# Two layers of cross-attention: the first image tokens of two entries in one tile of values

## The chip, the cores and the metric

The kernel runs on one core of a Trainium2 chip. The metric is the device time of one execution in microseconds (us), the median over some runs. A run's span, as the profiler shows it, goes from the first to the last instruction; the time has a little more around it.

The engines have these names in the profile: PE is TensorE's matmul, PEld its weight load, DVE VectorE, ACT ScalarE, POOL GpSimd, and SP the queue of SyncE, which issues nearly all DMAs of this kernel.

## The reference

B = 16 entries of S = 256 positions and C = 320 channels, in 20 heads of 16, pass through two layers. Each entry has 256 context tokens of E = 512 channels. In layer 0 the first 77 are text and the other 179 image tokens:

```python
q = hidden_states @ Wq
k_text, v_text = text @ Wk, text @ Wv
text_out = softmax(q_h @ k_h.T * scale) @ v_h
ip_k, ip_v = ip @ Wk_ip, ip @ Wv_ip
scores = q_h @ ip_k_h.T * scale
text_probs = softmax(q @ k_text.T * scale)            # over all channels, one per entry
sem = (text_probs @ text) @ ip.T * scale              # shared by the 20 heads
ip_probs = softmax(scores + 0.5 * sem) * spatial_mask[:, None]
out = (text_out + ip_probs @ ip_v_h) @ Wout + bout + residual
```

Layer 1 has 252 text tokens and 4 image tokens and normalises the two sides of its semantic term. All is in fp32.

## The kernel before

Each fp32 operand is split into a high and a low float32r half, and a product is the sum of three terms (high·high, high·low, low·high). So `prod` with kt = 4 blocks of 128 context channels issues 12 matmuls (line 325). The halves are made by `halves`: ACT copies the high half (L244), another engine subtracts (L245).

Layer 0 works on pairs of entries c = (2c, 2c+1), which share one context tile for each of the four blocks: `cta`, `cta`, `ctb`, `ctb`, each 128 x 2 halves x 512 columns, entry after entry, 77 text columns first in each. `context` loads the four raw blocks, one DMA of 128x512 each, and POOL and ACT split them. For each pair the tasks are:

- `keys0` (task k0): three blocks m of keys; for m = 0, 1 a product of the text columns (two entries by 96 columns, L325) and one of the image columns (two by 180), for m = 2 one product of all 512. The keys go through `kst` to memory, `kd`, by `keys_out`.
- `queries0` (q0), to memory `qd`.
- `tokens0` (m0t): the product of an entry's 77 text tokens with its image tokens, 77 x 192; its half, M, is part of the semantic term.
- `values0_` (v0): three products per entry, 128 tokens by 320 channels: tokens 0 to 127 with the text weights (`wC`), tokens 0 to 127 with the image weights (`wD`), tokens 128 to 255 with the image weights. ACT evacuates each into `vr`, the first two with a mask on the rows (`tmask`), with a column of ones after each head's 16 (V0W = 17 columns a head).
- `semantic0` (s0): the text probabilities of an entry; its first product is queries by text keys, 128 x (2 x 96) (L792), with the keys read back from `kd` into `kb`.
- `close0` (c0): the output projection (L725).

The attention itself runs in 80 slots, five groups g of four heads for each entry. A slot's K stack `ks` has 77 rows of M (broadcast to the four heads by ACT, L846), 48 rows of keys loaded from `kd`, and two rows of indicators (-1 for text, -1 for image columns); its Q stack `qs` has the text probabilities (ACT, L843), the queries, and the negative maxima. `stacks0` fills them, LEAD = 4 slots ahead. In a slot, `score0` makes S (L874), DVE takes the maxima (L875, L876), PE transposes them (L881), `turned0` makes the transposed scores T (L896), ACT their exp P (L899), POOL the product with the semantic factor rs (L902), and `attend0` the products with the values (L934). L820 is a product of an entry's semantic task.

PE runs in program order. What comes between a slot's own steps is set by the table STEPS: for each task the times, in slots, at which its steps are issued (negative: before the entry's first slot); `fill` runs the steps that are due. In layer 0 SP's instructions, too, stand in an order set when the program is built. The start, up to the first slot, is written out by hand in `begin`.

```python
def prod(out, lhs, rhs, kt):
    terms = [(k, a, b) for k in range(kt) for a, b in ((0, 0), (0, 1), (1, 0))]
```

## Time and profile before

| what | us |
|---|---|
| median of 3 runs (lowest, highest) | 1452.26 (1450.29, 1454.2) |
| the profiled execution, its time | 1451.59 |
| the profiled execution, its span | 1449.8 |
| busy: PE | 1401.7 |
| busy: PEld | 1157.8 |
| busy: DVE | 1174.2 |
| busy: POOL | 1152.3 |
| busy: ACT | 937.6 |

A row of a timeline has the start, the time, the engine, the line of the code, the operation, the tiles (out<-in), the shapes and how many instructions were merged; in brackets the idle time ahead of it and what ended that. The ends of matmuls are modelled, so the time of a run of matmuls is taken from its start to the start of what follows. A row of a group has the count, the busy us and the mean ns of one, and the idle time ahead of them. Layer 0 ends, and layer 1 begins, between 565 and 690 us.

### The profile page before, as it was taken

How to read it: one execution, taken by the hardware profiler on the slowest of the kernel's cores; microseconds unless marked ns; L12 is line 12 of the kernel's file. 1: busy time of each engine (PE TensorE's matmuls, PEld its weight loads, DVE VectorE, ACT ScalarE, POOL GpSimd, SP SyncE). 2: the span in 40 equal slices, each digit the busy share in tenths (PEclk: the TensorE clock that was granted, in tenths of full speed). 3: DMA queues.
4: the chain of work that ended last, by engine and by line, in shares of the span. 5: the costliest groups of instructions: out<-in, count | busy, mean ns of one | idle time of the engine just before them, and what ended most of it. 6: DMA issues, size and time to landing. Idle time of an engine off the chain costs nothing.

```text
span 1449.8 us, 35042 instructions
## 1 busy us (share of the span) xinstructions
PE 1401.7 (97%) x12166; PEld 1157.8 (80%) x12166; DVE 1174.2 (81%) x2570; ACT 937.6 (65%) x2075; POOL 1152.3 (79%) x1181
## 2 busy tenths in 40 slices
PE   7899999999999999889999999999999999999998
PEld 6788888888888888577777788878878888888865
DVE  5477777777777788867888888988998889888887
ACT  5567676767676776755666666666666666566553
POOL 4269797979787878887778887788778877887785
PEclk9999999999999999999999999999999999999999
DMA  6866575665656578575544444544454445444411
GB/s 200 197 161 181 143 186 147 163 169 155 168 151 171 145 201 232 133 188 155 158 123 124 143 141 125 154 137 140 130 150 138 139 135 149 139 136 131 130 33 50
DMA packets 236284, 215.74 MB, mean 149 GB/s; under 512 B 57834, under 2 KB 222732, under 8 KB 236108
## 3 DMA queue, kind: packets, MB, share of 16 engines
q1 hardware_dynamic: 233886, 212.53, 53.4%
q8 instruction: 97, 1.59, 0.5%
q10 hardware_dynamic: 2222, 0.98, 0.3%
q14 instruction: 79, 0.65, 0.2%
HBM read 127.32 MB, written 85.16 MB: 147 GB/s over the span
## 4 chain that ended last, share of the span: by engine, by line
PE 52%; DVE 3%; POOL 1%; issue 1%; ACT 0%; DMA 0%; ACTq 0%; DVEq 0%; POOLq 0%
PE X L1075 18%; PE X L325 9%; PE X L725 6%; PE P L1088 5%; PE T L1018 4%; PE S L1023 3%; PE P L1090 2%; PE X L1209 1%; PE X L651 1%; PE P L1055 1%; DVE mn L1024 1%; PE P L934 1%; POOL P L902 0%; DVE wt L1078 0%; POOL wt L1066 0%
## 5 line engine op out<-in xcount | busy, mean ns | idle before, releaser
L902 POOL TENSOR_TENSOR P<-P,rs 128x512 f32<-128x512 f32 x320 | 412.4, 1313 | 136.1 <-ACT P L899 136.0
L1075 PE MATMUL X<-ctb,gm 128*128 128x512 f32 x1120 | 293.3, 403 | 0.7 <-DVE wt L1078 0.7
L1066 POOL TENSOR_TENSOR wt<-P,ctb 128x512 f32<-128x512 f32 x212 | 268.1, 1293 | 0.0
L899 ACT ACTIVATE P<-T 128x512 f32<-128x512 f32 x320 | 174.7, 594 | 101.8 <-PE T L896 83.7
L1024 DVE TENSOR_REDUCE mn<-S 128x4 fp32r<-128x1008 f32 x160 | 192.1, 1200 | 58.7 <-PE S L1023 56.8
L1075 PEld LDWEIGHTS X<-ctb,gm 128*128 128x128 f32 x1120 | 202.5, 190 | 38.5 <-DVE wt L1078 0.9
L1078 DVE TENSOR_TENSOR wt<-X,wt 128x512 f32<-128x512 f32 x240 | 159.7, 682 | 4.2 <-PE X L1075 3.9
L1030 ACT ACTIVATE P<-T 128x512 f32<-128x512 f32 x212 | 115.2, 598 | 58.3 <-PE T L1018 56.6
L1080 POOL TENSOR_TENSOR wt<-wt 128x512 f32<-128x512 f32 x80 | 103.5, 1294 | 60.2 <-DVE wt L1078 60.0
L876 DVE TENSOR_REDUCE mn<-S 128x4 fp32r<-128x716 f32 x160 | 142.5, 890 | 0.0
L1065 ACT ACTIVATE ctb<-P 128x512 fp32r<-128x512 f32 x212 | 122.4, 625 | 29.4 <-PE X L1075 20.6
L934 PE MATMUL P<-P,vr 128*32 128x256 f32 x1920 | 123.7, 388 | 0.0
L725 PE MATMUL X<-ho,wF 128*128 128x256 f32 x768 | 109.0, 286 | 2.2 <-DVE ho L974 1.2
L725 PEld LDWEIGHTS X<-ho,wF 128*128 128x128 f32 x768 | 100.5, 189 | 8.8 <-DVE ho L974 2.7
L725 PE MATMUL X<-hq,wE 128*128 128x256 f32 x720 | 102.7, 286 | 4.6 <-ACT hq L706 3.3
L725 PEld LDWEIGHTS X<-hq,wE 128*128 128x128 f32 x720 | 96.4, 193 | 8.3 <-ACT hq L706 3.8
L875 DVE TENSOR_REDUCE mn<-S 128x4 fp32r<-128x308 f32 x160 | 74.8, 468 | 23.2 <-PE S L874 22.9
L945 DVE STREAM_TRANSPOSE nt<-P 128x512 f32<-128x512 f32 x80 | 57.1, 714 | 39.2 <-PE P L934 38.9
L934 PEld LDWEIGHTS P<-P,vr 128*32 128x32 f32 x1920 | 56.1, 110 | 40.8 <-issue 4.9
L874 PE MATMUL S<-ks,qs 125*128 125x256 f32 x480 | 85.7, 301 | 2.2 <-DMA ks<-kd 1.7
L874 PEld LDWEIGHTS S<-ks,qs 125*128 125x128 f32 x480 | 64.4, 189 | 28.2 <-issue 24.1
L325 PE MATMUL X<-cta,wA 128*128 128x252 f32 (+3 forms) x534 | 78.8, 292 | 7.9 <-ACT wA L244 5.7
(231 smaller groups left out, 3275.3 us busy)
## 6 DMA issues: line engine op xcount, KB each, us to landing
qd<-q SPq DMA_DIRECT2D x80, 256.0 KB
qs<-qd SPq DMA_DIRECT2D x160, 112.0 KB
ks<-kd SPq DMA_DIRECT2D x160, 112.0 KB
rawc<-in_cT_dram SPq DMA_DIRECT2D x60, 256.0 KB
kd<-kst SPq DMA_DIRECT2D x50, 256.0 KB
qs<-qd SPq DMA_DIRECT2D x60, 192.0 KB
ks<-kd SPq DMA_DIRECT2D x60, 192.0 KB
qd<-q SPq DMA_DIRECT2D x64, 128.0 KB
```

What stands on the lines that cost most here:

```text
L325: last = mm(out, lhs(a, k), rhs(b, k), start=i == 0, stop=i == len(terms) - 1)
L725: mm(pp, w(s, k, slice(m * 128, (m + 1) * 128)), a[:, t], start=i == 0, stop=i == len(terms) - 1)
L874: mm(sp[:, h], Q[: XROW + T0, h, t * 128 : (t + 1) * 128], K[: XROW + T0, h], start=True, stop=True)
L876: anchor(nc.vector.tensor_reduce(mn[:, 1, :, t], sp[:, :, T0:], axis=AX.X, op=ALU.max))
L899: exp = anchor(nc.scalar.activation(pt, st[p], AF.Exp, scale=SCALE))
L902: anchor(nc.gpsimd.tensor_mul(pt, pt, rs[:, t : t + 1].to_broadcast([128, 2, S])))
L934: mm(pv[32 * s : 32 * s + 32, o : o + S], v[:, vt, h : h + 32], P[k, s // 2][:, t, s % 2], start=vt < 2, stop=vt != 1,)
L1024: anchor(nc.vector.tensor_reduce(maxes[k + 2][:, :, t], sp[:, :, :T1], axis=AX.X, op=ALU.max))
L1065: nc.scalar.activation(R[k, u][:, t], P[k, u][:, t], AF.Copy, scale=0.5)
L1066: anchor(nc.gpsimd.tensor_sub(W[k, u][:, t], P[k, u][:, t], f(R[k, u][:, t])))
L1075: mm(yp, gm[:, gb], R[k, u][:, kt], start=i == 0, stop=i == len(blocks[n]) - 1)
L1078: nc.vector.tensor_mul(product, yp, w[:, n])
```

## The change

**The layout of a pair.** The context tile of a pair is PW = 538 columns wide: the even entry's text (0 to 76), the odd entry's image tokens (77 to 255), a gap of 26, the even entry's image tokens (282 to 460), the odd entry's text (461 to 537). In this layout 128 columns from 205 hold 51 image tokens of the odd entry, the gap, and 51 of the even one. `bring` loads a raw block of a pair with three DMAs (77, 179 and 256 columns); the first pair's is loaded in one DMA and put in place by the halves.

**Values.** The tile at 205 gives the first image values of both entries with one product, which ACT evacuates twice, with a mask for each, into both entries' `vr`. So a pair has five products where it had six, starting at columns 0, 410, 77, 205 and 333. `attend0` of the even entry makes sure that this product has been issued.

**Text keys and tokens.** The text keys' product has 156 columns (was 192), the tokens' 180 (was 192), the semantic product 154 (was 192). The text keys are evacuated in two pieces, one for each entry. An odd entry now has image tokens ahead of text in its keys.

**The stacks.** The two indicator rows lie in `kd`, written there at the start by six DMAs from memory to memory; a K stack loads 50 rows instead of 48, and nothing is copied from `mt` to `ks`. M is broadcast over all 256 columns (1024 with the four heads, was 716).

**Steps.** Numbers of STEPS moved, among them those of v0, m0, w7, t1 and o1. The opening loads wki ahead of the first wq and xq ahead of wv.

```diff
+GAP = 2 * T0 - 128
+PW = 2 * S + GAP
+CT, CI = (PW - T0, 0), (T0, S + GAP)
...
-    "m0e": (-7.4,),
-    "m0o": (-4.8,),
+    "m0e": (-8.2,),
+    "m0o": (-4.6,),
     "v0e": (-7, -5.2, -4.8,),
-    "v0o": (-4, -3.8, -3.4,),
+    "v0o": (-4.6, -4.4, -3.2,),
...
-    "t1": (-3.2, -2.2, -2.2, -1.4, -0.2,),
+    "t1": (-3.2, -2, -2, -1.2, 0,),
...
-    ("m0t", 2): (1.6,),
+    ("m0t", 2): (4.4,),
...
+    def bring(raw, src):
+
+        if src.shape[-1] == 2 * S:
+            for to, at, n in (0, 0, T0), (T0, S + T0, NI), (S + GAP, T0, S):
+                dma(raw[..., to : to + n], src[..., at : at + n])
+        else:
+            dma(raw, src)
...
-    ind0 = buf("raw", [128, 512], bufs=SIZES["RAW"], name="ind0")[:2, :S]
-    dma(ind0, ind0_d)
-    ind0r = buf("mt", [8, S], FR, name="ind0r")[:2]
-    nc.scalar.copy(ind0r, ind0)
+    for r in range(2):
+        for j, pieces in ((0, ((IM[0], IM[1]), (TX[0], TX[1]))), (1, ((slice(0, S), slice(0, S)),))):
+            for to, at in pieces:
+                rows = kd[0][:, (XROW + r) * H : (XROW + r + 1) * H, j, to]
+                dma(rows, ind0_d[r : r + 1, at].unsqueeze(1).to_broadcast([B // 2, H, to.stop - to.start]))
...
-        dma(ks[i][KS0 - 2 : KS0], ind0r.unsqueeze(1).to_broadcast([2, 4, S]))
...
+    def text_keys(c, kst, w, n):
+
+        kp = bank()[:n, : 2 * T0 + 2]
+        prod(kp.rearrange("p (b t) -> p b t", b=2), w, lambda s, k: of_pair(c, k, s, CT[1], CT[0] - CT[1] - 1, T0 + 1), 4)
+        text_rows(kst, (kp[:, :T0], kp[:, T0 + 2 :]), slice(0, n))
...
     def values0_(b):
-        ct, i = ct0[b // 2], b % 2
-        V = vr[(b + 2) % 3]
-        for t, (w,), lo, sc in ((0, wv0, 0, tmask[:, 0:1]), (1, wvi0, 0, tmask[:, 1:2]), (2, wvi0, 128, 1.0)):
+        j, ring = 1 - b % 2, lambda b: vr[(b + 2) % 3]
+        V = ring(b)
+        parts = [(0, wv0, (PW - 128, 0)[j], 1), (2, wvi0, (CI[0], CI[1] + NI - 128)[j], 0)]
+        nc.vector.tensor_copy(vcols(V, V0W)[:, 0:2, :, 16], vmasks[j].unsqueeze(2).to_broadcast([128, 2, H]))
+        if b % 2:
+            parts.insert(0, (1, wvi0, S + T0 - 128, 1))
+        for t, (w,), lo, masked in parts:
             vp = bank()[:, :320]
-            prod(vp, lambda s, k: ct(s, k)[:, i, lo : lo + 128], lambda s, k: w(s, k), 4)
-            nc.scalar.activation(
-                vcols(V, V0W)[:, t, :, 0:16], vp.rearrange("p (h d) -> p h d", d=D), AF.Copy, scale=sc
-            )
+            prod(vp, lambda s, k: ct0[b // 2][k][:, s, lo : lo + 128], lambda s, k: w(s, k), 4)
+            for i in (j,) if t != 1 else (1, 0):
+                scale = vmasks[i][:, t : t + 1] if masked else 1.0
+                nc.scalar.activation(
+                    vcols(ring(b - i if t == 1 else b), V0W)[:, t, :, 0:16], vp.rearrange("p (h d) -> p h d", d=D), AF.Copy, scale=scale
+                )
+            if t == 1:
+                results["mixed", b // 2] = True
             yield
         return V
...
     def semantic0(b):
...
-        NT = 96
+        NT = T0
...
-                dma(K[T0 : T0 + XROW], stack_rows(kd[0][b // 2][:, :, b % 2])[:, hs])
+                dma(K[T0 : T0 + XROW + 2], kd[0][b // 2][:, 1 - b % 2].rearrange("(q h) t -> q h t", h=H)[:, hs])
...
-                    m = f(get("m0t", b)[:, 0:1, T0:]).to_broadcast([T0, 4, S - T0])
-                    order(nc.scalar.copy(K[:T0, :, T0:], m), *casts[-1:])
+                    m = f(get("m0t", b)[:, 0:1]).to_broadcast([T0, 4, S])
+                    order(nc.scalar.copy(K[:T0], m), *casts[-1:])
...
     def attend0(k):
         b, g = divmod(k, NG)
         v, pv = get("v0", b), bank("P")
+        while ("mixed", b // 2) not in results:
+            step(("v0", b + 1))
```

Where instructions come to stand is shown at three places. First PE, in the steady part of layer 0, where the tokens and values of an odd entry are made; each row is an instruction of one term or several, `cta` and `ctb` the blocks of the context, `wC` and `wD` the text and image weights of the values, P the product of the attention. Before:

```order
L874 MATMUL S<-ks_193,qs_189 128x256 x4
L896 MATMUL T<-qsl,ksl 128x256 x4
L325 MATMUL X<-cta_82 77x192 x3
L325 MATMUL X<-cta_83 77x192 x3
L325 MATMUL X<-ctb_84 77x192 x3
L325 MATMUL X<-ctb_85 77x192 x3
L325 MATMUL X<-wD,cta_82 128x320 x3
L325 MATMUL X<-wD,cta_83 128x320 x3
L325 MATMUL X<-wD,ctb_84 128x320 x3
L325 MATMUL X<-wD,ctb_85 128x320 x3
L934 MATMUL P<-P_95,vr 32x256 x2
```

After:

```order
L346 MATMUL X<-cta_82 77x180 x3
L346 MATMUL X<-cta_83 77x180 x3
L346 MATMUL X<-ctb_84 77x180 x3
L346 MATMUL X<-ctb_85 77x180 x3
L346 MATMUL X<-wD,cta_82 128x320 x3
L346 MATMUL X<-wD,cta_83 128x320 x3
L346 MATMUL X<-wD,ctb_84 128x320 x3
L346 MATMUL X<-wD,ctb_85 128x320 x3
L346 MATMUL X<-wC_177,cta_82 128x320 x3
L346 MATMUL X<-wC_177,cta_83 128x320 x3
L346 MATMUL X<-wC_177,ctb_84 128x320 x3
L346 MATMUL X<-wC_177,ctb_85 128x320 x3
```

The wD product that opens the odd entry's values is now the one of both entries, and the wC product follows it at once; over layer 0 the rows with wD go from 384 matmuls to 288.

Second the queue of SP in the opening, from the last weight loads to the first keys on their way to memory (`mt` held the indicator rows, `kst` keys, `q` queries). Before:

```order
L139 DMA raw<-in_wvi_dram 128x320
L139 DMA ind_196<-in_ind_dram 2x256
L139 DMA ks_192<-mt_198 2x4x256
L139 DMA ks_193<-mt_198 2x4x256
L139 DMA ks_194<-mt_198 2x4x256
L139 DMA ksl<-mt_198 2x4x256
L139 DMA kd_66<-kst_237 128x2x256
L139 DMA kd_66<-kst_237 128x256
```

After:

```order
L145 DMA kd_66<-in_ind_dram 8x20x256
L145 DMA raw<-in_wv_dram 128x320
L145 DMA kd_66<-in_ind_dram 8x20x179 x2
L145 DMA kd_66<-in_ind_dram 8x20x77
L145 DMA raw<-in_wvi_dram 128x320
L145 DMA kd_66<-in_ind_dram 8x20x77
L145 DMA rawc_92<-in_wvi_dram 128x320
L145 DMA rawc_93<-in_wvi_dram 128x320
L145 DMA raw<-in_wvi_dram 128x320
L145 DMA xq_144<-in_xT_dram 128x3x256
L145 DMA kd_66<-kst_254 128x2x256
```

The indicator rows now go to `kd` between the loads of the value weights, and nothing stands between the last of these loads and the keys but one load of x.

Third the queue of SP in a steady pair, where the context of a later pair is loaded between the loads of the stacks. Before:

```order
L139 DMA rawc_93<-in_cT_dram 128x512
L139 DMA rawc_92<-in_cT_dram 128x512
L139 DMA qd_2626<-q_299 128x2x256
L139 DMA qd_2626<-q_299 128x256
L139 DMA ks_193<-kd_66 48x4x256
L139 DMA qs_189<-qd_1997 48x1024
```

After:

```order
L145 DMA rawc_93<-in_cT_dram 128x256
L145 DMA rawc_93<-in_cT_dram 128x179
L145 DMA rawc_93<-in_cT_dram 128x77
L145 DMA rawc_92<-in_cT_dram 128x256
L145 DMA rawc_92<-in_cT_dram 128x179
L145 DMA rawc_92<-in_cT_dram 128x77
L145 DMA qd_2651<-q_322 128x2x256
L145 DMA ks_213<-kd_66 50x4x256
L145 DMA qs_209<-qd_1974 48x1024
```

Six loads stand where two stood, ahead of the loads of the next stacks.

209 lines of the change are left out of this document (123 added, 86 removed), and 26 rows, old and new, of the table STEPS.

## Prediction

> **What bounds the kernel now.** I read the head of the page first, then the table by stretches, then the waits of the middle of layer 0, and last the timeline of TensorE (PE) and of the DMA queue (SP) at the places which the change touches. The head shows PE busy for 97% of the span, in front of DVE (81%), the weight loads (PEld, 80%) and POOL (79%).
>
> ```profile
> span 1449.8 us, 35042 instructions
> PE 1401.7 (97%) x12166; PEld 1157.8 (80%) x12166; DVE 1174.2 (81%) x2570; ACT 937.6 (65%) x2075; POOL 1152.3 (79%) x1181
> ```
>
> The table by stretches (core, then busy us and instructions of PE, PEld, DVE, ACT, POOL; then granted clock, DMA share, GB/s) tells where PE is the limit and where it isn't.
>
> ```profile
> 0.00:50.00 50.00, 37.91 (x227) 35.34 (x228) 24.29 (x65) 28.13 (x63) 17.80 (x37) 0.97 0.72 202
> 50.00:100.00 50.00, 44.06 (x368) 38.18 (x367) 34.04 (x70) 29.98 (x69) 25.26 (x21) 0.97 0.71 187
> ...
> 200.00:300.00 100.00, 100.00 (x932) 86.48 (x934) 74.78 (x183) 72.08 (x162) 86.88 (x78) 1.00 0.66 176
> ...
> 500.00:600.00 100.00, 94.83 (x883) 80.30 (x884) 82.03 (x196) 72.14 (x166) 81.24 (x77) 0.98 0.75 199
> 600.00:700.00 100.00, 89.44 (x807) 71.96 (x807) 75.83 (x159) 58.17 (x126) 79.96 (x79) 0.98 0.59 158
> 700.00:800.00 100.00, 96.22 (x796) 76.36 (x795) 89.08 (x177) 64.57 (x142) 81.82 (x86) 1.00 0.49 139
> ```
>
> In the middle of layer 0 PE has no gap at a clock of 1.00, so work taken off PE there is time. The opening leaves PE idle for 18 us, the transition between the layers (500 to 800) for 19.5 us; there, work on PE is worth only what the gaps don't swallow. A chain of other engines could hide behind a full PE, so I looked at who waits for whom from 200 to 500 (us in total, times, longest).
>
> ```profile
> POOL P L902 <- ACT P L899: 44.8, 44, 2.4
> ACT P L899 <- PE T L896: 43.6, 40, 1.8
> ```
>
> POOL waits for ACT and ACT for PE: the chain of a slot has its slack behind PE, not ahead of it. PE sets the pace.
>
> **The value products.** The timeline of PE in a steady pair (start, us, engine, line, names, shapes, count) prices one product.
>
> ```profile
> 302.04 0.29 PE L820 MATMUL X<-tph,M 77*128 77x256 f32 x1
> ...
> 308.11 0.70 PE L325 MATMUL X<-cta 128*77 128x192 f32 x6
> 308.64 0.69 PE L325 MATMUL X<-ctb 128*77 128x192 f32 x6
> 309.17 1.07 PE L325 MATMUL X<-wC,cta 128*128 128x320 f32 x6
> 310.08 1.04 PE L325 MATMUL X<-wC,ctb 128*128 128x320 f32 x6
> 310.95 0.22 PE L881 MATMUL X<-ident_r,mn 128*16 128x128 f32 x1
> ...
> 315.56 1.48 PE L792 MATMUL X<-kb,q 128*128 128x192 f32 x12
> 316.88 0.22 PE L881 MATMUL X<-ident_r,mn 128*16 128x128 f32 x1
> ...
> 526.77 0.28 PE L820 MATMUL X<-tph,M 77*128 77x256 f32 x1
> ```
>
> A value product starts at 309.17 and the next instruction at 310.95: 1.78 us for 12 matmuls of 320 columns, 148 ns each. Six products a pair become five, so a pair gives back 1.78 us. The two L820 rows lie six entries (three pairs) apart, so a pair takes 224.73/3 = 74.9 us.
>
> **Tokens, text keys, semantic scores.** The token product (12 matmuls, 77 weight columns, 192 moving) takes 309.17 − 308.11 = 1.06 us; at 180 columns, in proportion, 0.07 us less, twice a pair: 0.13 us. Text keys go from 192 to 156 columns and semantic scores from 192 to 154, 24 matmuls of each a pair. The semantic product L792 takes 316.88 − 315.56 = 1.32 us for the same 192 columns which cost the token product 1.06. What differs is the weights, 128 columns against 77: at 128 weight columns a short product is paced by its load, not by the columns that stream. So I count nothing for the shorter columns there. The bounds are 0 and the token product's rate, 1.06/12/192 = 0.46 ns a column: 24 × (36 + 38) × 0.46 = 0.82 us a pair. I take 0, since L792 is the product itself and the token rows only its neighbour.
>
> Together 1.9 us a pair. Seven pairs (the second to the eighth) are computed under a full PE, or nearly so: 13.3 us. The eighth pair's products fall partly into 500 to 600, where PE idles 5.17 us, so up to 1.9 of the 13.3 is less sure. The first pair's is in the opening, below.
>
> **What is added in the steady stretch.** The groups by form (count, then busy us and mean ns) price it.
>
> ```profile
> L843 ACT CAST qs<-tph 77x1024 fp32r<-77x1024 f32 x48 | 49.8, 1039 | 0.0
> L846 ACT CAST ks<-M 77x716 fp32r<-77x716 f32 x48 | 37.7, 785 | 0.0
> ...
> L245 POOL TENSOR_TENSOR cta<-rawc,cta 128x512 fp32r<-128x512 f32 x44 | 56.1, 1294 | 0.0
> ```
>
> The copy of M into the K stack grows from 716 to 1024 columns, so to the L843 row: 8 a pair by 254 ns, 2.0 us. With three more split key evacuations ACT gets about 2.7 us a pair; it goes from 72% of 74.9 to some 78% of 73. POOL's context halves grow by 26 of 512 columns: 4 × 66 ns = 0.26 us a pair; POOL goes from 87% to about 89%. DVE's share stays below 80%. None reaches PE's share, and the cover is the 44 us that POOL and ACT wait for each other in 300 us. If the cover fails, the exps come late and PE waits for P. I allow 1 us for new stalls, 0 to 4 over the layer.
>
> SP issues three context loads for each one: 8 more a pair by about 0.45 us (0.91/2, in the rows below), 3.6 us of issue in 73. Behind them in the queue stand the K and Q loads of the stacks, each well ahead of its use, as the timeline shows:
>
> ```profile
> 308.30 0.33 SPq L139 DMA_DIRECT2D ks<-kd  x1
> ...
> 316.93 0.69 PE L874 MATMUL S<-ks,qs 125*128 125x256 f32 x4
> ```
>
> 8.6 us from issue to use. A burst of three context loads in place of one is 0.9 us more, two such bursts 1.8; that fits.
>
> **The opening.** SP issues in a row here, and PE waits twice for its loads.
>
> ```profile
> 24.51 2.29 SPq L139 DMA_DIRECT2D ks<-mt  x3
> ...
> 33.20 3.65 SPq L139 DMA_DIRECT2D kd<-ho x6
> ...
> 38.36 0.33 SPq L139 DMA_DIRECT2D ks<-kd  x1
> ...
> 40.92 0.91 SPq L139 DMA_DIRECT2D rawc<-in_cT_dram  x2
> 42.63 1.63 SPq L139 DMA_DIRECT2D raw<-in_cT_dram  x2
> 45.24 3.67 SPq L139 DMA_DIRECT2D kd<-kst  x4
> 49.01 3.74 SPq L139 DMA_DIRECT2D kd<-ho  x6
> 52.86 0.70 SPq L884 DMA_DIRECT2D qs<-mt  x1
> ...
> 44.16 0.71 PE L874 MATMUL S<-ks,qs 125*128 125x256 f32 x4 [1.67 <-DMA ks<-kd]
> ...
> 54.96 0.71 PE L896 MATMUL T<-qs,ks 127*128 127x256 f32 x4 [3.13 <-DMA qs<-mt]
> ```
>
> The indicator copies ks<-mt (2.29 us and one more) leave this place, and six DMAs from memory to memory take over earlier, between the weight loads. Each kd<-ho group has four issues for six, 1.2 us less (3.65/6 × 2). The first S follows ks<-kd and can come 1.2 us earlier, up to 3 if the removed copies also held up the queue; PE's wait there is 1.67, so no more than that is gained at once. The first T follows qs<-mt, which has stood behind the context loads and both key groups: 1.2 to 1.7 earlier by the first S, 1.2 by the shorter group, 8 × 0.35 to 0.45 = 2.8 to 3.6 later by the longer loads, of which the queue's own pauses between 41.83 and 45.24 (1.8 us free of issues) cover all or nothing. That is −1.9 to +1.2 for T. The pair's product saved, 1.78, lies ahead of this wait and counts only if T's wait vanishes. The six memory copies are the unknown: at one to two issues (0.45 to 0.9 us) behind wv or wvi they delay a value product, which has room until 44. I take −1 for the opening, nearer the early end since the pauses are there, and from −4 to +3.
>
> **Moved steps.** Numbers of STEPS move by up to 2.8 slots (m0t of entry 2) but mostly by a few tenths; a step moved under a full PE changes who is first, not the sum. In the transition and in layer 1 the products are the same ones in another order: 0, from −2 to +2. The steps of the mixed product are pulled ahead of the first value step of the even entry, so the odd entry's ring buffer is taken early; three buffers serve two entries, and the next taker comes five slots later.
>
> **The sum.** The profiled execution took 1451.59 us. −13.3 − 1 + 1 + 0 = 1438.3; the median of the three runs is 0.67 above the profiled execution, so 1439.0 us. A difference of about 0.3%, 4.4 us, is what a measurement of this kernel can tell from none: faster means under 1447.9, slower over 1456.6.
>
> **The rivals.**
>
> The first: *odd weight columns.* The mixed tile and two others begin at columns 205, 77 and 333 of a 4-byte tile, where before all began at 0 or 128. If such a load took longer, 36 matmuls a pair would pay. At twice the 110 ns (1.32/12) by which L792 is paced, a matmul would take 220 ns for 148: 36 × 72 = 2.6 us a pair against 1.9 saved. That is 7 × 0.7 = +4.9, about 1457. It cancels the gain from 53 ns a load. Against it stand the rows of the attention products, whose weights start at multiples of 17 columns in layer 0 (half of them odd) and of 22 in layer 1 (all even):
>
> ```profile
> L934 PEld LDWEIGHTS P<-P,vr 128*32 128x32 f32 x1920 | 56.1, 110 | 40.8 <-issue 4.9 <-POOL hq L707 1.0 <-POOL P L902 0.3
> ...
> L1088 PEld LDWEIGHTS P<-P,v1t 128*32 128x32 f32 x848 | 22.1, 109 | 16.5 <-issue 0.4
> ```
>
> 110 against 109 ns: odd starts cost nothing at 32 columns. Chance 0.05.
>
> The second, the one on the slower side: *the K load gets late.* It carries 50 rows where it carried 48. Its only bound in the rows is the first one, issued at 38.36 and waited for until 44.16: 5.8 us at most. The steady cushion is 8.6. So a load half as long again (8.7) just uses it up, and each further 0.2 us in some 70 slots eats the whole 13.3. At 1.6 times, 9.3 us, S is 0.7 late in each slot: 49 us on top of 1439, about 1488. For it: the DMA share is 0.66 already, and the last step of the score hangs on it. Against: 5.8 includes the wait for the writes of kd, so the load is shorter. Chance 0.06. The Trainium skill, "DMA: Bandwidth & Descriptors", section "Why a DMA increments its semaphore by 16 and not by 1", says that a transfer runs on the largest number of engines up to 16 that divides its slowest dimension: 48 rows on 16, 50 on 10, the factor 1.6 by estimate. No row of this profile shows the number of engines of one load.
>
> The third: *shorter columns pay after all.* The 0.82 us of the upper bound by 7 pairs is 5.7 us more: 1433. Against it stands the 1.32 of L792. Chance 0.09. The Trainium skill, "TensorE: Matmul & The Clock Gate", section "Back-to-back issue gap", gives N/2.4 + 2.5 ns for N columns alone, which would say 82 ns at 192, and adds that at small N it undercounts for want of the load; L792 agrees with the addition, at 110.
>
> The fourth: *the transition takes the gain back.* Layer 0 ends 13 us earlier, while the casts of layer 1's weights and contexts on ACT, POOL and DVE, which PE waits for between 500 and 800, don't come earlier: if half of the gain returns as idle time, 1446; if all, 1452. For it: 19.5 us of idle are there now. Against: no other engine is above 90% in these stretches, and the same steps are due by slot, so they move up with the layer. Chance 0.14, half of it within 0.3%.
>
> **Chances and range.** The forecast has 0.66. Faster: 0.66 + 0.09 + 0.07 = 0.82. Same: 0.07 + 0.03 of the first rival = 0.10. Slower: the rest of the first, 0.02, and the second, 0.06: 0.08. The forecast's own range is 1434 to 1446 by the opening (−4 to +3), the stalls (0 to 4) and the transition (±2). To leave out two in ten I reach to the third rival below and to the fourth above: 1430 to 1449.
>
> **What would show it.** In the profile after, the two wD groups of L325 have 144 matmuls where these have 192:
>
> ```profile
> L325 PE MATMUL X<-wD,cta 128*128 128x320 f32 x192 | 33.7, 310 | 0.0
> L325 PE MATMUL X<-wD,ctb 128*128 128x320 f32 x192 | 33.3, 309 | 0.0
> ```
>
> The pair's period falls from 74.9 to about 73.0, with PE still at 100% between 200 and 500. The 12 matmuls of a product at an odd column still take 1.78 us; 2.6 would show the first rival. Twelve semantic matmuls still take about 1.3; 1.1 would show the third. Any wait of PE for ks<-kd after 100 us would show the second. Idle time of PE from 500 to 800 well above 19.5 us would show the fourth. The first T should come at 53 to 55; a T past 58 would mean that I took the context loads too lightly. A wait of PE on P (L902) in the steady stretch would say that ACT's 2.7 us were not hidden.

## The result: slower by 1.2%

The changed kernel takes 1469.78 us (median of 4 runs, 1468.62 to 1472.09) against 1453.08 before (4 runs beside it, 1450.29 to 1454.2): a ratio of 1.0119, 95% interval 1.0100 to 1.0139. The forecast was 1439.0, from 1430 to 1449, with 0.82 on faster. The sign was wrong.

The profiled execution has a span of 1466.8 us against 1449.8. The head of its page:

```profile
span 1466.8 us, 34987 instructions
PE 1396.1 (95%) x12070; PEld 1149.3 (78%) x12070; DVE 1193.0 (81%) x2618; ACT 951.4 (65%) x2106; POOL 1152.4 (79%) x1185
```

PE has 96 matmuls fewer and 5.6 us less busy time, and yet the span is 17 us longer: PE waits more. The table by stretches, with the columns of the one before, shows where:

```profile
0.00:50.00 50.00, 32.89 (x195) 30.20 (x196) 23.60 (x77) 28.31 (x70) 17.84 (x41) 1.00 0.70 192
50.00:100.00 50.00, 41.69 (x328) 37.47 (x327) 30.33 (x62) 26.06 (x62) 17.83 (x15) 0.90 0.70 186
...
200.00:300.00 100.00, 96.78 (x921) 82.26 (x919) 76.35 (x181) 73.48 (x163) 86.28 (x77) 1.00 0.65 173
...
500.00:600.00 100.00, 95.53 (x882) 81.84 (x883) 80.19 (x189) 74.56 (x166) 81.81 (x76) 0.98 0.77 204
600.00:700.00 100.00, 88.92 (x819) 69.96 (x816) 80.08 (x171) 63.87 (x138) 85.23 (x84) 0.97 0.61 159
700.00:800.00 100.00, 94.75 (x774) 74.83 (x772) 82.94 (x161) 59.56 (x128) 77.21 (x81) 0.97 0.44 130
```

From 200 to 300 PE was full before and now idles 3.2 us. The opening idles 25.4 us (18 before), at a mean clock of 0.95 (0.97 before). From 500 to 800 it idles 20.8 (19.5 before), at a clock lower by up to 0.03.

Where the time goes is read best from the starts of the same slots, taken from the first matmul of T in each (us; 60 is the first slot of the thirteenth entry, 90 lies behind the transition):

| slot | before | after | later by | of it since the row above |
|---|---|---|---|---|
| 0 | 54.96 | 60.94 | +5.98 | +5.98 |
| 5 | 102.20 | 108.54 | +6.34 | +0.36 |
| 20 | 213.88 | 220.64 | +6.76 | +0.42 |
| 60 | 510.87 | 524.52 | +13.65 | +6.89 |
| 90 | 761.82 | 779.00 | +17.18 | +3.53 |
| 159 | 1418.61 | 1436.54 | +17.93 | +0.75 |
| end of the span | 1449.81 | 1466.84 | +17.03 | −0.90 |

So there are three losses: 6 us in the opening, 7 in four steady pairs (75.97 us for one against 74.24), 3.5 in the transition. The waits of PE from 200 to 500 (us in total, times, longest) had no row before and now have three, each once a pair:

```profile
PE X L346 <- DVE tmp L1029: 5.6, 4, 1.4
PE X L346 <- DVE ho L1050: 2.4, 4, 0.6
PE P L1012 <- POOL P L977: 2.3, 4, 0.6
```

In starts of matmuls these are gaps of 1.72, 0.87 and 0.97 us, where before no gap above 0.33 stands. Less the 0.15 to 0.3 that lies between two starts anyway, they cost 2.7 to 3.1 us a pair. The products save 1.9, and a pair is 1.7 longer, so some 0.5 to 0.9 us of the loss stand in no gap of this size.

### The copy that waits for POOL

The first of the three waits on the timelines of PE, DVE and POOL in the changed kernel:

```profile
338.09 1.06 PE L346 MATMUL X<-wD,ctb 128*128 128x320 f32 x6
340.55 1.11 PE L346 MATMUL X<-wC,cta 128*128 128x320 f32 x6 [1.40 <-DVE tmp L1029]
```

```profile
334.78 1.35 DVE L570 COPY vr<-vmask 128x40 f32<-128x40 f32 x1 [0.22 <-PE P L1012]
336.03 0.70 DVE L1023 STREAM_TRANSPOSE nt<-P 128x512 f32<-128x512 f32 x1
...
340.00 0.41 DVE L1029 TENSOR_TENSOR tmp<-nt,P 128x256 f32<-128x256 f32 x1
340.33 0.41 DVE L1050 TENSOR_TENSOR ho<-X,ho 128x256 fp32r<-128x256 f32 x1
```

```profile
334.77 5.02 POOL L977 TENSOR_TENSOR P<-P,rs 128x512 f32<-128x512 f32 x4 [0.41 <-ACT P L974]
```

PE waits at 340.55 for DVE, by its row until the operation on `tmp` is done; DVE has worked without a pause since 334.78. At the head of that chain stands a copy of 40 elements a partition, 1.35 us long. It starts with the first of POOL's four operations (334.77), and DVE's next instruction starts at 336.03, when that operation (5.02/4 = 1.26) ends. The second wait has the same form: the copy takes 1.22 from 299.62, and POOL's two operations run from 298.26 to 300.79.

```profile
299.62 1.22 DVE L570 COPY vr<-tmask 128x40 f32<-128x40 f32 x1 [0.47 <-PE P L1012]
300.75 0.22 DVE L259 TENSOR_TENSOR kst<-X,kst 128x77 fp32r<-128x77 f32 x1
```

```profile
298.26 2.53 POOL L977 TENSOR_TENSOR P<-P,rs 128x512 f32<-128x512 f32 x2 [0.63 <-ACT P L974]
```

All sixteen copies by their source line (shortest, median, longest ns, then first and last start):

```profile
L570 DVE COPY vr<-tmask x8: 194/1216/1228, 14.4 to 528.7; 128x40 f32<-128x40 f32 x8
L570 DVE COPY vr<-vmask x8: 196/1347/1351, 49.1 to 565.6; 128x40 f32<-128x40 f32 x8
```

The copy by itself takes 0.2 us: so long last the two that meet an idle POOL, at 39.98 and 49.14. Thirteen start while POOL works on a product P (L977), and every one of them ends 0.06 to 0.07 us after that operation, also the three that start late in it and last only 0.48 to 0.70 us. This is the line of the diff that fills the column of ones, `nc.vector.tensor_copy(vcols(V, V0W)[:, 0:2, :, 16], ...)`, once for each entry.

### The profile page after: what moved, and what is told of

Its sections match the earlier page's. It is cut to its first block, busy times and chain, and to the rows that moved or that the text cites. A ratio compares the mean times of both kernels' runs of the same rounds, so it can differ in the third digit from the quotient of the medians.

```text
span 1466.8 us, 34987 instructions
## 1 busy us (share of the span) xinstructions
PE 1396.1 (95%) x12070; PEld 1149.3 (78%) x12070; DVE 1193.0 (81%) x2618; ACT 951.4 (65%) x2106; POOL 1152.4 (79%) x1185
## 4 chain that ended last, share of the span: by engine, by line
PE 80%; DVE 8%; DMA 3%; POOL 3%; issue 2%; ACT 2%; SPq 1%; ACTq 0%; DVEq 0%; POOLq 0%
PE X L346 17%; PE X L1153 17%; PE X L798 11%; PE P L1012 7%; PE S L948 5%; PE P L1166 5%; PE T L1096 4%; PE T L971 4%; PE S L1101 3%; PE P L1168 2%; POOL P L977 1%; SPq L145 1%; PE X L1287 1%; DVE mn L951 1%; POOL wt L1144 1%
## 5 line engine op out<-in xcount | busy, mean ns | idle before, releaser
L977 POOL TENSOR_TENSOR P<-P,rs 128x512 f32<-128x512 f32 x320 | 410.2, 1306 | 139.9 <-ACT P L974 139.7
L1012 PE MATMUL P<-P,vr 128*32 128x256 f32 x1920 | 126.9, 386 | 5.7 <-POOL P L977 4.8
L346 PE MATMUL X<-wC,cta 128*128 128x320 f32 x480 | 81.0, 315 | 7.0 <-DVE tmp L1029 7.0
```

What stands on the lines that cost most here:

```text
L346: last = mm(out, lhs(a, k), rhs(b, k), start=i == 0, stop=i == len(terms) - 1)
L977: anchor(nc.gpsimd.tensor_mul(pt, pt, rs[:, t : t + 1].to_broadcast([128, 2, S])))
L1012: mm(pv[32 * s : 32 * s + 32, o : o + S], v[:, vt, h : h + 32], P[k, s // 2][:, t, s % 2], start=vt < 2, stop=vt != 1,)
```

## The experiments

Most of these kernels were executed once, and their times are compared with one execution of the kernel before on the same chip (1450.88 to 1452.45; for the indicator copies with the median of 16, 1452.84). How far they carry is seen from the last kernel, which was profiled twice: its slots 20 to 60 took 292.50 and 292.52, its slot 5 came at 109.43 and 107.17, its stretch from slot 60 to 90 took 255.18 and 257.53, and that from 90 to 159 657.28 and 658.81. So a steady pair is good to 0.02 us, the opening and the transition only to about 2.4, layer 1 to about 1.5.

### The copy of the ones: on ACT, and alone on DVE

```diff
-        nc.vector.tensor_copy(vcols(V, V0W)[:, 0:2, :, 16], vmasks[j]...
+        nc.scalar.copy(vcols(V, V0W)[:, 0:2, :, 16], vmasks[j]...
```

> The changed kernel with one edit: the copy that sets the column of ones in vr runs on ACT, not on DVE. Theory A: in the changed kernel this copy of 40 elements takes 1.2 to 1.35 us on DVE in the steady part of layer 0 (0.19 us in the opening), and the evacuations behind it on DVE free the banks of PSUM late; the two gaps of PE that follow it (1.72 us ahead of a wC product, 0.87 ahead of a wB product, 2.3 us a pair over their usual 0.15) go, a pair falls from 75.97 to about 73.7 us, and the run from 1470 to about 1456. Theory B (the moved steps make the evacuations late): the gaps stay, a pair stays at 76.0, 1470. A copy on ACT of 1 us or more would say that the place of the writing, not DVE, costs the time.

Measured: 1459.22, 10.6 under the changed kernel's median and 3 above what was expected. The pair goes from 75.97 to 73.94. The copies take 0.25 us, and of the three waits from 200 to 500 the two behind DVE's chain are gone:

```profile
L570 ACT COPY vr<-tmask x8: 251/254/265, 14.4 to 522.4; 128x40 f32<-128x40 f32 x8
L570 ACT COPY vr<-vmask x8: 243/257/267, 48.9 to 559.9; 128x40 f32<-128x40 f32 x8
```

```profile
PE P L1012 <- POOL P L977: 2.4, 4, 0.6
PE S L948 <- DVE mn L951: 1.8, 4, 0.5
```

The other way round, the kernel before with such a copy added for each entry:

```diff
         V = vr[(b + 2) % 3]
+        nc.vector.tensor_copy(vcols(V, V0W)[:, 0:2, :, 16], tmask[:, 0:2].unsqueeze(2).to_broadcast([128, 2, H]))
```

> The kernel before with one part of the change alone: a copy on DVE of 40 elements a partition into the columns of ones of vr, once an entry (the same values that stand there already). Theory: on DVE it takes 1.2 us and more while POOL works, and PE, which is full here, gets waits of up to 2 us a pair: a pair of 75 to 76.3 instead of 74.24, 1456 to 1465. Rival (the copy only hurts with the change's other order): the copy takes 1.2 us, but a pair stays at 74.3, 1453.

Measured: 1454.06 against 1452.45, a pair of 74.73 (+0.49): under the 75 of the theory, above the 74.3 of the rival.

```profile
L504 DVE COPY vr<-tmask x16: 196/207/1467, 15.3 to 557.4; 128x40 f32<-128x40 f32 x16
```

Here eight of the copies meet an idle POOL and take 0.2 us; five last 1.46, and these too end 0.06 us after one of POOL's operations. So the copy costs what the place of POOL's operation makes of it: 2.0 us a pair in the changed kernel, 0.5 in the one before.

### The moved steps

`STEPS` of the kernel before in the changed kernel; then the same with the ones on ACT.

> The changed kernel with the table STEPS of the kernel before, all else changed. Theory A (copy on DVE): a pair in the steady part keeps gaps of PE of some 2 us or more, near 76 us; layer 1, whose work is the same, goes back to 48.1 us an entry from 48.4 if its own numbers of STEPS made the difference: some 4 us less there, 1466. Theory B (moved steps): a pair falls to about 72.4 us (74.24 less 1.9), and the run to about 1452.

> The copy on ACT as in e1, and the table STEPS of the kernel before. If the moved steps cost something in the steady part, a pair falls below e1's 73.95, to 72.4 to 73.3, and layer 1 runs at 48.1 us an entry instead of 48.4. If they are worth something now that DVE is free of the copy, a pair is at 74 or more. In the run with before's STEPS alone a pair took 75.3 against 75.97, so I expect about 73.3 and, with an opening later by 3 us, the same time as e1: 1459.

Measured: 1472.61 and 1467.06 (1466 and 1459 were expected); pairs of 75.28 and 74.69 on average from slot 20 to 60. With the old table the steady pair is 0.7 faster beside the DVE copy and 0.75 slower without it, so the moved numbers aren't the loss. But they set what the copy costs: with the old table it is worth 0.6 us a pair (75.28 to 74.69), with the new one 2.0. Layer 1, slots 90 to 159, goes back from 657.54 to 656.68 and 656.71 (656.79 before): its 0.75 us are the moved steps. All seven executions here with the old table took 655.4 to 656.8 there, all thirteen with the new one 657.2 to 658.8.

### POOL's gap

The third wait stands behind POOL: after two halves of the context (L259) it does four products P in a row, and PE waits for the last.

```profile
358.31 2.64 POOL L259 TENSOR_TENSOR ctb<-rawc,ctb 128x538 fp32r<-128x538 f32 x2
360.92 0.45 POOL L1034 TENSOR_TENSOR hsn<-tmp 128x128 f32<-128x128 f32 x1
361.34 5.20 POOL L977 TENSOR_TENSOR P<-P,rs 128x512 f32<-128x512 f32 x4
```

Two attempts, both with the ones on ACT. One issues a step of k0 later (−12 to −11.4), the other lets DVE subtract the last of a pair's four halves:

```diff
-                halves(*ahead.pop(0), eng, wait)
+                last = eng is nc.gpsimd and i == len(parts) and parts[-1][0].shape[-1] == 2 * S
+                halves(*ahead.pop(0), nc.vector if last else eng, wait)
```

> The copy on ACT as in e1, and one number of STEPS moved: the fifth time of k0 from -12 to -11.4, so that POOL's two halves of ctb don't stand next to each other. In e1 a pair takes 73.95 us, with a gap of PE of 0.97 us ahead of a P matmul that waits for POOL, behind these two halves (2.64 us), and one of 0.82 where S waits. Theory (POOL's own order makes the rest of the loss): the 0.97 gap goes and the pair falls to about 73.2 us. Rival (POOL has simply no slack over these slots: 9.4 us of work in the slot of 9.1): the wait moves to another place and the pair stays at 73.9.

> The copy on ACT as in e1, and the low half of a pair's last context block made on DVE, not on POOL. In e1 POOL is busy for 22.6 us in three slots of 22.45 (slots 47 to 49), behind two halves in a row. Theory (POOL is the bound there): with 1.3 us less on POOL the gap of 0.97 ahead of a P matmul goes, and perhaps part of the 0.82 one: a pair of 72.8 to 73.3 instead of 73.95. Rival (the wait isn't POOL's amount of work): 73.9 or more.

The later step gave 1472.18 and pairs of 76.5, where 73.2 was hoped for: PE now waits at the text keys for that half, and DVE runs late behind it.

```profile
PE X L346 <- DVE sp L869: 4.6, 3, 1.5
PE X L956 <- DVE mn L951: 3.0, 3, 1.0
PE X L346 <- POOL ctb L259: 2.6, 4, 0.7
```

The half on DVE took the wait for POOL away; pairs of 73.13, 0.8 less than with the ones on ACT alone. One row is left from 200 to 500:

```profile
PE S L949 <- DVE mn L952: 1.8, 4, 0.5
```

Its time, 1459.16, is nonetheless that of the kernel with the ones on ACT (1459.22): the 3.2 us won from slot 20 to 60 are lost by slot 20 (+1.8) and from 60 to 90 (+1.7), both inside what two executions of one kernel differ by.

### The opening

SP in the opening of the changed kernel, from the loads of pair 1's context to the first load for T:

```profile
43.45 6.69 SPq L145 DMA_DIRECT2D rawc<-in_cT_dram  x6
50.51 3.52 SPq L145 DMA_DIRECT2D raw<-in_cT_dram  x6
54.08 1.95 SPq L145 DMA_DIRECT2D kd<-kst  x4
56.07 2.59 SPq L145 DMA_DIRECT2D kd<-ho  x4
58.76 0.77 SPq L959 DMA_DIRECT2D qs<-mt  x1
```

The twelve context loads hold SP from 43.45 to 54.03, 10.6 us, where four held it from 40.92 to 44.26. The issues themselves are not longer, 0.33 to 0.43 us each; between them SP waits for earlier DMAs to land (its waits from 43 to 59):

```profile
SPq L145 <- DMA ks<-kd: 4.3, 3, 1.8
SPq L145 <- DMA qs<-qd: 1.0, 2, 0.7
SPq L145 <- DMA xq<-in_xT_dram: 0.5, 1, 0.5
```

In both programs a DMA of SP waits on the semaphore that it is going to use, until the DMA eight places ahead of it in the queue has landed; these pauses end 0.016 us after that landing. Before, the same waits (for ks<-kd, qs<-qd and xq) came partly behind the context loads, among the key writes, so the loads cost less than it looks: from its first load of K to qs<-mt SP takes 17.24 us (41.52 to 58.76) where it took 14.50 (38.36 to 52.86), 2.7 us more. The other 3.2 us are there before that first load. The shorter key group takes 2.59 for 3.74, the 1.2 us less that were foretold; so the eight more loads cost some 3.9. PE's waits follow, 3 us later on ks<-kd and 6 on qs<-mt:

```profile
47.19 0.71 PE L948 MATMUL S<-ks,qs 125*128 125x256 f32 x4 [2.06 <-DMA ks<-kd]
...
60.94 1.19 PE L971 MATMUL T<-qs,ks 127*128 127x256 f32 x4 [6.13 <-DMA qs<-mt]
```

Two kernels put one part each into the kernel before: three DMAs for each context load, and six copies of the indicator rows (into a spare place in memory).

```diff
-                dma(raw, src)
+                if shape[-1] == 2 * S:
+                    for lo_, hi_ in ((0, T0), (T0 + S, 2 * S), (T0, T0 + S)):
+                        dma(raw[..., lo_:hi_], src[..., lo_:hi_])
+                else:
+                    dma(raw, src)
```

```diff
+    spare = dram.tile([B // 2, 2 * H, 2, S], F32, name="spare")
+    for r in range(2):
+        for j, pieces in ((0, (slice(0, S - T0), slice(S - T0, S))), (1, (slice(0, S),))):
+            for to in pieces:
+                dma(spare[:, r * H : (r + 1) * H, j, to], ind0_d[r : r + 1, to]...
```

> The kernel before with one part of the change alone: each context load of the pairs after the first is issued as three DMAs (77, 179 and 256 columns) into the same contiguous place. Theory (loads): the four loads of the opening then take 6 to 10 us of SP instead of 2.5, qs<-mt stands behind them, and the first T comes at 58 to 61 instead of 54.96; slot 5 comes 4 to 6 us late (106 to 108 instead of 102.2); in the steady part a pair stays at 74.24. 1456 or so. Rival (the opening's loss comes from the other edits there): T at 56 or earlier, slot 5 at 103, 1452.

> The kernel before with one part of the change alone: six copies of the indicator rows from memory to memory, of the change's sizes, into a spare place that nothing reads, among the value weights' loads; ks<-mt stays as it was. Theory (their 0.65 MB delay what is loaded behind them): the last load of wvi, for which ACT waits 3.06 us before (until 23.67), lands 2 to 4 us later, the first S at 46 to 48 instead of 44.16, slot 5 1 to 3 us late; 1453 to 1456. Rival (the copies are free, and the q of the changed kernel is late by ACT's order alone): first S within 1 us of 44.16, slot 5 within 1 us of 102.2.

The split loads: 1455.89, first T at 59.91 (+4.95), slot 5 +4.8, a pair 74.24, as the theory had them; from the first load of K to qs<-mt SP takes 19.46 us. SP's rows:

```profile
40.86 5.46 SPq L139 DMA_DIRECT2D rawc<-in_cT_dram  x6
47.24 4.55 SPq L139 DMA_DIRECT2D raw<-in_cT_dram  x6
```

The indicator copies: 1459.8 (1456 at most was expected), first S at 47.04 (+2.9), first T at 58.22 (+3.3), slot 5 +3.7. Here SP reaches its first load of K at 42.25, 3.9 us late, and goes on from there as before (13.85 to qs<-mt). Part of this is chance: two products of the keys run at half clock, from 29.81 to 33.23, and take 1.6 us more. Another 4.2 us are lost between slots 5 and 20, 3.3 of them in one wait of PE for DVE that the changed kernel hasn't. Either part alone does over half of the damage by slot 5; in the changed kernel the two give 6.3, not 8.5. In this second kernel the first queries come when they came before (18.0 for 17.8), in the changed one at 22.05, behind a cast of ACT: that delay isn't made by the copies alone. With the copies moved or split (the first and the third of the next four) it is 20.48 and 19.66.

Taking parts out of the changed kernel again was less clear. Indicator copies behind the weight loads; pair 1's context in four DMAs; only pair 0's indicators ahead; pair 1's loads behind the first T's:

> The changed kernel with one edit: the six copies of the indicator rows from memory to memory are issued after the weight loads and the second load of x (SP is idle there from 23.6 to 31.0 us), not between the value weights' loads. Theory A: they held up the loads of wv and wvi (the last landed at 20.7 where 15 was usual), ACT's queue waited for these, and so the first query product began at 22.05 us instead of 17.81; it now begins near 18.5, the first S comes at 44 to 45 instead of 47.19, and the first T 3 us earlier, at 58; the run is 3 us shorter, 1467. Rival: the queue's order in ACT (the hq cast behind the wC casts) alone makes q late, and the first q stays near 21.

> The changed kernel with one edit: the second pair's context, loaded in the opening, comes with one DMA for each block (four, not twelve) and is put in place by the halves, three for each block on ACT and DVE. Theory A: the twelve issues took 10.2 us of SP (43.45 to 54.03) where four took 2.5, and the first T waits behind them for qs<-mt; it comes at 54 to 55 instead of 60.94, PE's 6.13 us wait there shrinks to about 1, and the run is 5 us shorter, 1465. Rival: T is late because the first S is, by 3 us, and the queue only fills the time: T comes at 58 or later.

> The changed kernel with one edit: the opening writes the indicator rows of the first pair alone (six small copies at the same place); those of the other seven pairs are written at the end of the opening. Theory (the 0.65 MB that these copies move through the DMA engines delays the weight loads): first query product at 19 to 20 us instead of 22.05, first S at 45 instead of 47.19. Rival (their six issues and not their bytes delay SP): unchanged, 22 and 47. Either way the whole moves by less than 3 us.

> The changed kernel with one edit in the opening: the second pair's context loads (twelve DMAs) are issued behind qs<-mt and not ahead of the key groups kd<-kst. Theory (the loads, by their place and their bytes, hold up qs<-mt): qs<-mt is issued at 52 or earlier instead of 58.76, the first T comes at 53 to 54 instead of 60.94; the second pair's keys come some us later, so that of the 7 us perhaps half is left by slot 5 (105 instead of 108.5): 1466. Rival (the bound is the writing of the keys themselves): T at 57 or later.

| kernel | time | first T | slot 5 |
|---|---|---|---|
| changed | 1469.78 | 60.94 | 108.54 |
| indicators late | 1470.84 | 60.41 | 110.14 |
| pair 1 in four DMAs | 1471.66 | 59.26 | 108.56 |
| indicators split | 1472.28 | 58.72 | 111.44 |
| loads behind qs<-mt | 1471.22 | 57.05 | 111.22 |

The split indicators do at the first S what was expected, 45.32 for 47.19. With pair 1 in four DMAs and with the loads behind, T comes as late as the rivals had it, and none of the four shortens the run: T comes 0.5 to 3.9 us earlier, and slot 5 not at all. What takes it back can be seen. With the loads behind, the next S waits 2.88 us for ACT's exp, which stands behind the casts of these loads. And the stretch behind T falls into a slow TensorE. In the changed kernel PE idles from 54.8 to 60.9, and the granted clock drops (stretches of 5 us, same columns, clock third from the end):

```profile
55.00:60.00 5.00, 0.00 (x0) 0.00 (x0) 1.69 (x3) 1.23 (x3) 0.00 (x0) 0.70 0.69 215
60.00:65.00 5.00, 4.06 (x19) 4.09 (x20) 1.97 (x3) 2.40 (x5) 2.51 (x2) 0.50 0.79 242
65.00:70.00 5.00, 5.00 (x34) 5.00 (x34) 4.23 (x11) 2.91 (x8) 0.00 (x0) 0.77 0.93 157
```

That is some 10 us at half the clock, of which 6.3 lie behind the first T; before, the same view shows 0.72 and 0.94 from 65 to 75 only, some 3.4 us. From T to slot 5 the kernel before takes 47.24 us, with PE idle for 4.0. With the loads behind these are 54.17 us, 7.8 idle and 11.6 at half clock; in the kernel below whose T comes earliest, at 52.52, 57.40 us, 10.9 idle and 10.2 at half clock. Its longest waits there:

```profile
PE S L966 <- ACT P L992: 2.8, 1, 2.8
PE X L816 <- ACT P L992: 2.1, 1, 2.1
```

So both waits for ACT and the clock give an earlier T back; no run takes either away, and what would bring slot 5 forward stays open.

### The wide copy of M

> The kernel before with one part of the change alone: the copy of M into the K stack takes all 1024 columns (716 before). My prediction counted 2.0 us more of ACT a pair and at most a little for it. If it is hidden, a pair stays at 74.24 and the run at 1452 to 1453; if exps come late because of it, a pair of 74.6 or more.

```diff
-                    m = f(get("m0t", b)[:, 0:1, T0:]).to_broadcast([T0, 4, S - T0])
-                    order(nc.scalar.copy(K[:T0, :, T0:], m), *casts[-1:])
+                    m = f(get("m0t", b)[:, 0:1]).to_broadcast([T0, 4, S])
+                    order(nc.scalar.copy(K[:T0], m), *casts[-1:])
```

Measured in the kernel before: pairs of 74.24, the same to 0.01: ACT hides it in the steady part, as the prediction had it. But 1459.94 against 1451.64, since slots 60 to 90 take 259.16 for 250.95. That is more than two executions differ by, and most of it is clock: 0.95, 0.94 and 0.98 in the three stretches from 500 to 800, for 0.98, 0.98 and 1.00. Between these slots 23.9 us ran at half clock for 6.8, and of the 8.2 us PE's busy time has 6.6. The kernel with the ones on ACT has the wide copy too and takes 252.24 there, so the copy alone doesn't make this.

### Mended together

The ones on ACT throughout; then the indicators split and late with pair 1 in four DMAs; these and the half on DVE; these and the loads behind the first T's; and only the half on DVE with pair 1 in four DMAs, the one that was executed twelve times more.

> The copy on ACT as in e1, and three edits of the opening together: the indicator rows of the first pair after the weight loads, those of the others at the end of the opening, and the second pair's context with one DMA for each block. Alone each brought the first T forward (60.41, 58.72, 59.26 against 60.94), but none slot 5 (110.1, 111.4, 108.6 against 108.5). Theory (the queue of SP and its bytes are the bound all through the opening): together T comes at 55 to 56 and slot 5 at 104 to 105 instead of e1's 110.3: 1453. Rival (slot 5 hangs on something else, as the casts that are split in the opening): slot 5 at 108 or later, 1457.

> The changed kernel with four repairs: the copy of ones on ACT (e1), the low half of the last context block on DVE (e9), the second pair's context with one DMA a block, the indicator rows of all but the first pair at the end of the opening (e10). If the parts add up: a pair of 73.1 us, slot 5 at about 109, and the run at 1454 to 1457. If the clock's dips in the opening fall otherwise than in e10, up to 3 us either way.

> As f1, and the second pair's context loads behind qs<-mt (as in e7). If the queue of SP ahead of qs<-mt bounds the opening to the end, the first T comes at 53 to 55 and slot 5 at 106 to 107: 1451 to 1454. If what it gives is taken back by the casts of those loads on ACT, as in e7 (2.9 us there), slot 5 stays at 109 or 110: 1454 to 1457.

> As f1 without the edit of the indicator rows. e4 and e10 differ by it (and by the copy on ACT): slot 5 at 108.6 and 109.8. If the indicator rows cost nothing by slot 5: the same as f1 within 1.5 us. If they cost what they take at the first S (2 us): f1 is 2 us ahead.

> The best of the repaired versions (copy of ones on ACT, fourth context half on DVE, one DMA a block for the second pair), timed against the kernel before. One look gave 1457.15 against 1451.64. Expected: 1455 to 1459, a ratio of 1.003 to 1.005, so still slower than before: 1.1 us a pair gained over before in the steady part, 7 lost in the opening, 4 in the transition.

| kernel | time | first T | slot 5 | 20 to 60 | 60 to 90 |
|---|---|---|---|---|---|
| before | 1453.08 | 54.96 | 102.20 | 296.99 | 250.95 |
| changed | 1469.78 | 60.94 | 108.54 | 303.88 | 254.48 |
| ones on ACT | 1459.22 | 61.85 | 110.28 | 295.75 | 252.24 |
| and the opening | 1461.97 | 56.94 | 109.78 | 295.65 | 256.09 |
| opening, half on DVE | 1459.87 | 56.41 | 109.70 | 292.64 | 256.43 |
| and the loads behind | 1459.64 | 52.52 | 109.92 | 292.55 | 257.42 |
| half on DVE, four DMAs | 1457.15 | 60.59 | 109.43 | 292.50 | 255.18 |
| the same, timed | 1456.07 | 59.51 | 107.17 | 292.52 | 257.53 |

The pairs came as expected (73.1), the times of the first three 2.6 to 5.0 us above the highest that was. The last takes 1456.07 (median of 12 runs) against 1452.84 (16 runs): a ratio of 1.0022, 95% interval 1.0011 to 1.0033; 1.003 to 1.005 was expected. So the mended change is still a little slower than the kernel without it: four pairs are 4.5 us faster, the opening is 5 to 7 us later, and slots 60 to 90 take 4 to 7 us more. No version of the change beat the kernel before.

## Why the prediction was wrong

**The saving itself: right.** The wD groups have 144 matmuls, as foretold:

```profile
L346 PE MATMUL X<-wD,cta 128*128 128x320 f32 x144 | 25.7, 314 | 0.0
L346 PE MATMUL X<-wD,ctb 128*128 128x320 f32 x144 | 25.2, 310 | 0.0
```

A wD product, which now always starts at an odd column, takes 1.77 us (47.74 to 49.51 in PE's timeline), for 1.78 before, and 1.78 to 1.83 in the steady pairs of the kernel with the half on DVE (1.77 to 1.87 before): the first rival is out. Semantic matmuls went from 110.0 to 108.6 ns by their starts, text keys from 117.7 to 116.9, tokens from 88.8 to 85.0: the third rival is out, and taking 0 for the shorter columns was right. PE nowhere waits for ks<-kd after the opening: the second rival is out. The load did get longer, 4.13 us from issue to landing (median, 200 to 500) for 3.52, but stays inside the cushion of 8.6. The rule of the Trainium skill, "DMA: Bandwidth & Descriptors", section "Why a DMA increments its semaphore by 16 and not by 1", would have put that load of 50 rows on fewer engines; the trace fits this, with 11 updates of the semaphore for each load of 50 rows and 16 for each of 48, but the time grew by a factor of 1.17, not 1.6.

**The steady stretch: the failed step is a term that was never in the sum.** Of the 30 us between forecast and result some 19.5 are here, 7 in the opening and 3.5 in the transition. "What is added" listed ACT's copies, POOL's columns and SP's issues, and passed over `nc.vector.tensor_copy`, one line of the diff shown. Of DVE it said only that its share stays below 80%. The pair, in measured terms: −1.9 for the products, +2.0 for the copy (gone with it on ACT), +0.8 for POOL's run of work (gone with a half on DVE), and +0.8 left in the mended pair (73.13 for 74.24), of which the wait for DVE's maxima is 0.5 and 0.3 stands behind no gap: +1.7 a pair, 6.9 in four, instead of the −1.9 and the allowance of 1 us in all. These prices hold in this order of steps; with the old table the copy costs 0.6. The pair of 74.9 that the sum started from was read too long as well: its two L820 rows span pairs of 74.24, 74.27 and 76.22, the last of them already at the end of the steady part. Had I listed the copy, I would still have counted it at its 0.2 us; only the rule below prices it at the rest of a POOL operation.

The Trainium skill, "SBUF — State Buffer", section "SBUF: two separate sides", says that VectorE in a two-port mode and GpSimd share one pair of ports as an exclusive lock held for a whole instruction, the loser waiting for all of it, and names the fp32 `tensor_copy` inside SBUF as such a case. The traces agree: 0.2 us with POOL idle, up to 1.35 us ending with POOL's operation, 0.25 us on ACT. That the lock is the cause is the reading of the Trainium skill; the runs show the coincidence of the ends and that the cost goes away on ACT.

**POOL's cover: the view was too coarse.** I took POOL at 87% from stretches of 100 us. In the pair's last three slots it already stood at 96% before (20.66 of 21.47), behind 80% in the seven ahead of them; now it is at 99%:

```profile
362.36:415.16 52.80, 52.80 (x493) 45.59 (x492) 38.29 (x91) 37.05 (x82) 42.39 (x39) 1.00 0.58 146
415.16:436.63 21.47, 21.47 (x210) 18.76 (x208) 16.56 (x41) 16.50 (x38) 20.66 (x19) 1.00 0.77 204
```

```profile
426.10:448.56 22.46, 21.87 (x210) 18.71 (x208) 16.95 (x42) 17.07 (x39) 22.15 (x20) 1.00 0.75 195
```

The first two rows are the kernel before (slots 40 to 46 and 47 to 49), the last the changed one (47 to 49). The 44 us of waiting which I called the cover lie in other slots.

**The opening: mis-sized and of the wrong sign.** The sum let the first S come 1.2 us earlier and gave the indicator copies "room until 44"; S came 3.0 later. The copies added alone give +2.9, and with them split, 1.9 of the 3.0 goes (45.32). The split loads at 2.8 to 3.6 us were nearly right (3.9 in the changed kernel, 5.0 added alone, 1.3 of it one slow issue), but the queue's pauses, which were to cover up to 1.8 of them, are waits for earlier DMAs to land and cover nothing. So −1 (from −4 to +3) was +6. The text named a T past 58 as the sign that the loads were taken too lightly; T came at 60.94, but half of that is the late S, so the sign was true in part by luck.

**The transition.** 0 from −2 to +2 was +3.5. Of all kernels run here, none has slots 60 to 90 as short as the one before; they take 0.8 to 8.2 us more. With two executions of one kernel 2.4 apart, the runs don't put the 3.5 down to a part of the change. Most of it goes with the clock: between these slots 17.1 us ran at half clock for 6.8 before, PE's busy time grew by 2.6 us and its idle time by 0.9. The fourth rival, that the transition takes a gain of layer 0 back, is what the mended kernels look like: −4.5 from slot 20 to 60, +4.2 and +6.6 from 60 to 90, of which 3.2 and 3.5 are idle time of PE and the rest busy time, at 13.7 and 17.1 us of half clock.

**Moved steps.** "0" holds for the steady part on the whole; layer 1 lost 0.75 by them.

## What to carry to other kernels

Walk the diff line by line and give every added instruction a row in the sum, with the engine it is queued on and what runs on the engine beside it: a copy of 0.2 us on VectorE cost 2 us a pair because it met GpSimd's operations. Judge cover at the grain of the schedule (a slot), not over 100 us, and in an opening find out what a pause of the DMA queue waits for before it is taken as free. Where, as here, other engines are nearly as full as the one that binds (POOL at 96% in three slots of ten), a saving on that engine is an upper end, not the middle.

## What was not expected of the hardware

A VectorE copy of 40 elements a partition lasts 194 to 207 ns beside an idle GpSimd; beside a GpSimd tensor operation of 1.3 us it lasts until that is over, up to 1.35 us in the changed kernel and 1.47 in the one before with the copy. SP issues a context load in 0.33 to 0.43 us, but holds each back until the DMA eight places ahead has landed, and in the opening loads of K took 5.4 to 8.7 us to land. And the TensorE clock can stay at half for 10.2 us at a stretch: in the changed kernel around a wait of PE of 6.1 us, in the one with T at 52.52 behind a wait of 2.8 us, with PE busy for 9.9 of the 10.2. So the length of the wait doesn't tell that of the slow stretch. The Trainium skill, "TensorE: Matmul & The Clock Gate", section "Part 1: The HAM clock gate (the "warmup" mystery)", describes such a gate with windows of about 3.4 us, and the traces agree in this, that the slow stretches seen here last 3.4, 6.8 or 10.2 us.
